# Query and key projections by seven products of quarters instead of eight, in three PSUM banks

## The chip, the cores and the metric

The kernel runs on one core of a Trainium2 chip. The metric is the time of one execution on the device in microseconds (us). A core has five engines that work side by side, each through its own list of instructions in order: TensorE (PE, matmuls; its weight loads are listed apart as PEld), VectorE (DVE), ScalarE (ACT), GpSimd (POOL) and SyncE (SP, which issues most DMA transfers). They meet at semaphores. Matmuls write PSUM, which has banks of 128 partitions by 512 float32; everything else is in SBUF.

## The reference, cut to what matters

An input x of 2 batches of 1024 tokens and 1024 features is normalized and goes through one attention layer and, beside it, a gated feed-forward layer whose weights are stored in 4 bits. The change lies in the projections ahead of the attention:

```
h = layernorm(x)                       # (2, 1024, 1024)
q = rope(h @ wq)                       # 32 heads of 32, 1024 columns
k = rope(h @ wk)                       # 8 heads of 32, 256 columns
v = h @ wv                             # 256 columns, no rope
attention = softmax(q @ k.T / sqrt(32), causal) @ v @ wo
```

Four query heads share a key head. Rope turns neighbouring columns of a head by an angle that depends on the token: t * cos + swapped(t) * sin.

## The kernel before, in words

The two batches go one after the other through the stages "normalize", `project`, `attend` and `project_out`; the feed-forward layer comes last, for both. The stage that the change touches is `project`, called once a batch.

Normalized activations stand transposed in `xnT`: features on the partitions, in NS = 8 slices of 128, and 1024 tokens along the row, taken as two blocks of TB = 512. The weights of 128 columns are a tile of 8 slices of 128x128. For one block of 128 columns and 512 tokens, a **group**, PE runs eight float32 matmuls 128x512, one for each slice, that add up in one bank (L384). Three banks called ps_qk take turns. Keys have two blocks of columns, queries eight (NC), each with two blocks of tokens: 20 groups a batch, 160 matmuls.

After each group comes its **turn** (L386 to L398): DVE multiplies the bank by the cosines (L388) and shuffles neighbouring rows of the bank (L390), POOL multiplies the shuffled copy by the sines (L391) and adds the two (L392), ACT makes a rounded copy, `rot_hi` (L394), DVE subtracts it to get the rest, `rot_lo` (L396), and SP stores both to a DRAM buffer of queries or keys, `qs` or `ks` (L397, L398). From there the attention fetches them as stacks of rows, `room_*`.

Three other things are woven into `project`:

- `work`, the row maxima for the first group of heads (`head.rows()`): products of queries and keys, called s (L548 and L554), in two banks of their own, each followed by a DVE reduce (L564); 42 of these groups a batch. One is drawn after every second matmul of a query group from the third block of columns on. They need the first stacks, fetched after the keys and after the first query block (`head.keys()`, `head.queries()`).
- `side`: in batch 0 a survey of the 4-bit scales and zero points (`look`), whose transfers zb_gu (8) and zb_d (21) are issued from ACT's queue; in batch 1 the unpacking of 4-bit weights (`unpack`, DVE L258 to L263, ACT L267, POOL's transfers L249). `behind(turn)` asks the scheduler to put these behind the turn.
- after each query block, the split of one slice of xnT into x_hi (ACT, L439) and x_lo (DVE, L440), stored for the feed-forward layer.

At the end the values: 8 groups ps_v of 8 matmuls 128x256 (L407), copied out by ACT (L410).

Weights come from a pool of three tiles (`load_w`), loaded two blocks ahead. The order of instructions on each engine is set by a scheduler from the order of the program and these hints. `room` is nine tiles of 128x1024, allocated at once (L1457); the last four are filled only in `attend`. `oT`, where the attention leaves its result, is 128x8x1024 and idle during `project` (L1450).

Of the kernel before, what the change touches and what calls it, by code (L numbers as in the profile page):

```python
# [10 lines left out]
F32 = mybir.dt.float32  # L11
F32R = mybir.dt.float32r
# [5 lines left out]
AF = mybir.ActivationFunctionType  # L18
ALU = mybir.AluOpType
# [4 lines left out]
P = 128  # L24
# [8 lines left out]
NREP = N_HEADS // N_KV  # L33
# [3 lines left out]
def block_kernel(  # L37
# [18 lines left out]
    nc = tc.nc  # L56
# [288 lines left out]
    def load_w(pool, w_dram, c, **kw):  # L345
        return load_w_at(pool, w_dram, c, **kw)[0]
# [5 lines left out]
    def load_kv(pool, w_dram, w=None):  # L352

        if w is None:
            w = pool.tile([P, NS, N_KV * HD], F32, name="w_kv")
        nc.sync.dma_start(w, w_dram.rearrange("(g p) n -> p g n", p=P))
        return w

    def project(b, xnT, w_k, qs, ks, v, side, head):


        with tc.tile_pool(name="qkv_w", bufs=3, reuse_waits="tile") as wp, tc.tile_pool(name="qkv", bufs=3, reuse_waits="tile") as pool, tc.tile_pool(
            name="qkv_t", bufs=1, reuse_waits="tile"
        ) as tp, tc.tile_pool(name="qkv_ps", bufs=3, space=PSUM, reuse_waits="tile") as psp, tc.tile_pool(
            name="v_ps", bufs=2, space=PSUM, reuse_waits="tile"
        ) as vps, tc.tile_pool(name="x_split", bufs=2, reuse_waits="tile") as xp:
            cs = tp.tile([P, 2, T], F32, name="cs")
            for j in range(4):
                nc.sync.dma_start(cs[HD * j : HD * (j + 1)], rope.rearrange("a d t -> d a t"))
            swap = [i ^ 1 for i in range(32)]  # L370

            def behind(turn):

                order = ExitStack()
                for i in turn:
                    order.enter_context(tc.issue_after(i.ins))
                return order

            def turned(w, dst, work=iter(()), blocks=range(NB)):
                for n in blocks:  # L380
                    tok = slice(n * TB, (n + 1) * TB)
                    ps = psp.tile([P, TB], F32, name="ps_qk")
                    for s in range(NS):
                        nc.tensor.matmul(ps, w[:, s, :], xnT[:, s, tok], start=(s == 0), stop=(s == NS - 1))  # L384
                        if s % 2:
                            next(work, None)  # L386
                    t1 = pool.tile([P, TB], F32, name="rot1")
                    nc.vector.tensor_tensor(t1, ps, cs[:, 0, tok], ALU.mult)  # L388
                    t2 = pool.tile([P, TB], F32, name="rot2")
                    nc.vector.stream_shuffle(t2, ps, swap)  # L390
                    nc.gpsimd.tensor_tensor(t2, t2, cs[:, 1, tok], ALU.mult)  # L391
                    turn = [nc.gpsimd.tensor_tensor(t1, t1, t2, ALU.add)]  # L392
                    hi = pool.tile([P, TB], F32R, name="rot_hi", bufs=2)
                    turn.append(nc.scalar.copy(hi, t1))  # L394
                    lo = pool.tile([P, TB], F32R, name="rot_lo", bufs=2)
                    turn.append(nc.vector.tensor_tensor(lo, t1, hi.bitcast(F32), ALU.subtract))  # L396
                    nc.sync.dma_start(dst[0, :, tok], hi.bitcast(F32))  # L397
                    nc.sync.dma_start(dst[1, :, tok], lo.bitcast(F32))  # L398
                    with behind(turn):
                        for _ in range(3 if b else 1):  # L400
                            next(side, None)
                return turn
# [9 lines left out]
            wanted = list(range(NC))  # L412
            loaded = [load_w(wp, wq, wanted.pop(0)) for _ in range(2)]
            def following():
                if wanted:
                    loaded.append(load_w(wp, wq, wanted.pop(0)))
                return loaded.pop(0)


            for n in range(NB):  # L420
                for c in range(2):
                    turned(w_k[:, :, c * P : (c + 1) * P], ks[c], blocks=[n])
            w = load_kv(None, wv, w_k)
            head.keys()
            work = head.rows()
            for c in range(NC):
                turn = turned(following(), qs[c], work if c > 1 else iter(()))
                if c == 0:
                    head.queries()
                if c == NC - 2:  # L430

                    warm = tp.tile([P, 1], F32, name="warm")
                    nc.scalar.activation(warm, eps, AF.Exp)
                for n in range(NB):
                    tok = slice(n * TB, (n + 1) * TB)
                    hi = xp.tile([P, TB], F32R, name="x_hi")
                    lo = xp.tile([P, TB], F32R, name="x_lo")
                    with behind(turn):
                        nc.scalar.copy(hi, xnT[:, c, tok])  # L439
                        nc.vector.tensor_tensor(lo, xnT[:, c, tok], hi.bitcast(F32), ALU.subtract)  # L440
                    nc.sync.dma_start(xs_dram[b][0, :, c, tok], hi.bitcast(F32))
                    nc.sync.dma_start(xs_dram[b][1, :, c, tok], lo.bitcast(F32))

            for t in range(NT):
                next(work, None)
                values(t)
            for _ in work:
                pass
# [5 lines left out]
    class Clock:  # L454
# [6 lines left out]
        def product(self, w, n=1.0, switch=False):  # L461
            self.pe += 15.0 + 0.416 * n * w + (90.0 if switch else 0.0)
# [984 lines left out]
    for b in range(B):  # L1447
        keep_open = ExitStack()
        keep = keep_open.enter_context(tc.tile_pool(name="keep", bufs=1, reuse_waits="tile"))
        oT = keep.tile([P, NS, T], F32, name="oT")  # L1450
        q0_open = ExitStack()
        q0p = q0_open.enter_context(tc.tile_pool(name="at_q0", bufs=1, reuse_waits="tile"))
        with tc.tile_pool(name="at_first", bufs=1, reuse_waits="tile") as fp, tc.tile_pool(
            name="qkv_T", bufs=1, reuse_waits="tile"
        ) as qp:

            room = [q0p.tile([P, T], F32R, name=f"room_{j}") for j in range(1 + 2 * NREP)]  # L1457
            v = qp.tile([P, NT, N_KV * HD], F32, name="v")
            with tc.tile_pool(name="ps_s", bufs=1, space=PSUM, reuse_waits="tile") as ps_s:
                head = Maxima(qs_dram[b], ks_dram[b], fp, ps_s, room)  # L1460
                if b == 0:
                    with tc.tile_pool(name="prep", bufs=1) as pool, tc.tile_pool(
                        name="prep_ps", bufs=1, space=PSUM
                    ) as psp:
                        first = look(pool, psp)
                        project(b, xnT, w_k, qs_dram[b], ks_dram[b], v, first, head)
                        for _ in first:
                            pass
                else:
                    with tc.tile_pool(name="unpack", bufs=2, side="right", reuse_waits="tile") as up:  # L1470
                        side = unpack(up, range(8, 20), False)
                        project(b, xnT, w_k, qs_dram[b], ks_dram[b], v, side, head)
                        for _ in side:
                            pass
                x_open.close()
                output = Output(b, oT, q0p)
                attend(head, v, oT, output)
        if b == B - 1:
            ffn_args = start_ffn(ffn_open)
            xnT = xp = None  # L1480
        else:
            x_open, xnT, xp = open_x()
        with tc.tile_pool(name="unpack", bufs=3, side="right", reuse_waits="tile") as up:
            side = unpack(up, range(8) if b == 0 else range(20, NF), b == B - 1)
# [62 lines left out]
```

## Time and profile before

| what | value |
|---|---|
| runs of the kernel | 2291.7, 2293.06, 2296.47 us; median 2293.06 us |
| profiled execution | 2293.33 us, its span 2291.6 us |
| granted TensorE clock, mean | 0.993 |
| `project`, batch 0, first ps_qk to last ps_v | 26.9 to 220.4 us |
| `project`, batch 1, the same | 667.8 to 852.9 us |
| one group of 8 matmuls, PE, by the timeline | 6.87 us |

The span runs from the first to the last instruction. Rows of the profile name a line of the kernel, the engine, the operation, what it writes and reads, and the shape; then busy time in us and mean ns of one, then idle time ahead of it on its engine and what ended that. A float32 matmul leaves two records, so 160 matmuls a batch show as 320. Matmul records overlap, so that their mean is longer than the distance from one to the next.

### The profile page before, as it was taken

The numbers are of one execution on the slowest core, as the hardware profiler recorded it, in microseconds if no ns is written. First come the engines' busy times: TensorE is split into PE (matmuls) and PEld (weight loads), VectorE is DVE, ScalarE is ACT, GpSimd is POOL, SyncE is SP. The second block draws the span as 40 slices with busy tenths as digits, with TensorE's granted clock in tenths as the row PEclk, the third lists the DMA queues.
The fourth block names the chain that finished last, engine by engine and source line by source line (L and its number), as shares of the span: only waits on it lengthen the run. The fifth ranks groups of instructions, "written<-read, shape, count | busy, mean of one in ns | idle before, by whom it ended". The sixth has DMA issues, their size and how long they took to land.

```text
span 2291.6 us, 30825 instructions
## 1 busy us (share of the span) xinstructions
PE 2239.3 (98%) x11313; PEld 1537.5 (67%) x11313; DVE 1420.2 (62%) x2268; ACT 1132.3 (49%) x1819; POOL 792.4 (35%) x569
## 2 busy tenths in 40 slices
PE   7989999999999999999999999999999999999998
PEld 4455555555874465555558888888877888888875
DVE  5544677773324736777722367667877777777775
ACT  2102544553223325445533455555887555556875
POOL 1303677774035427776741100000234100001362
PEclk9999999999999999999999999999999999999999
DMA  5727323122468971231319623231846655323475
GB/s 180 220 91 244 80 47 93 38 75 76 129 210 280 301 215 47 52 88 38 80 54 344 181 56 83 55 83 55 303 138 219 176 137 139 96 71 105 137 231 154
DMA packets 262183, 309.50 MB, mean 135 GB/s; under 512 B 19147, under 2 KB 197707, under 8 KB 261880
## 3 DMA queue, kind: packets, MB, share of 16 engines
q1 hardware_dynamic: 245172, 260.62, 38.4%
q0 software_dynamic: 10752, 38.02, 5.2%
q10 hardware_dynamic: 6100, 8.82, 1.2%
q8 instruction: 91, 1.49, 0.3%
q14 instruction: 68, 0.56, 0.1%
HBM read 214.58 MB, written 97.03 MB: 136 GB/s over the span
## 4 chain that ended last, share of the span: by engine, by line
PE 82%; issue 7%; POOL 6%; DVE 2%; ACT 2%; DMA 1%; SPq 0%; ACTq 0%; POOLq 0%; DVEq 0%
PE acc L1198 27%; PE acc L1079 12%; PE ps_wo L880 10%; PE st L661 7%; PE s L554 7%; PE o L708 5%; PE ps_qk L384 5%; PE l L726 3%; PE st L676 2%; PE ps_v L407 1%; POOL rot L391 1%; PE s L548 1%; POOL rot L392 1%; POOL p L821 1%; ACT p L686 1%
## 5 line engine op out<-in xcount | busy, mean ns | idle before, releaser
L1198 PE MATMUL acc<-x,w 128*128 128x512 f32 x2752 | 640.1, 393 | 1.2 <-ACT gate L1169 0.9
L1198 PEld LDWEIGHTS acc<-x,w 128*128 128x128 f32 x2752 | 512.3, 188 | 120.5 <-DVE h L1171 7.2
L564 DVE TENSOR_REDUCE mx<-s 128x1 f32<-128x512 f32 (+3 forms) x672 | 384.8, 608 | 190.3 <-PE s L554 91.7
L968 DVE TENSOR_SCALAR acc<-acc,r_gu 128x1024 f32<-128x1024 f32 x301 | 389.1, 1293 | 166.5 <-PE acc L1198 164.9
L686 ACT ACTIVATE p<-st 128x512 f32<-128x512 f32 (+3 forms) x768 | 314.7, 497 | 316.8 <-PE st L676 314.6
L966 ACT ACTIVATE acc<-acc,r_gu 128x1024 f32<-128x1024 f32 x301 | 327.4, 1088 | 231.5 <-PE acc L1198 226.7
L1182 POOL TENSOR_TENSOR h_lo<-h,h_hi 128x512 fp32r<-128x512 f32 x78 | 100.3, 1287 | 805.2 <-DVE h L1160 300.6
L821 POOL TENSOR_TENSOR p<-p 128x2048 f32<-128x2048 f32 (+3 forms) x122 | 360.0, 2955 | 9.0 <-PE o L708 4.6
L968 DVE TENSOR_SCALAR acc<-acc,r_d 128x512 f32<-128x512 f32 x320 | 241.7, 759 | 62.0 <-PE acc L1079 59.3
L966 ACT ACTIVATE acc<-acc,r_d 128x512 f32<-128x512 f32 x320 | 210.8, 663 | 61.8 <-PE acc L1079 55.0
L384 PE MATMUL ps_qk<-xnT,w_qk 128*128 128x512 f32 x512 | 236.0, 602 | 2.5 <-DVE rot L390 2.5
L880 PE MATMUL ps_wo<-oT,w_o 128*128 128x256 f32 x1024 | 232.1, 382 | 0.0
L1079 PE MATMUL acc<-h_lo,w 128*128 128x512 f32 (+1 forms) x576 | 228.9, 397 | 3.0 <-POOL h_lo L1182 2.6
L1079 PE MATMUL acc<-h_hi,w 128*128 128x512 f32 (+1 forms) x576 | 229.5, 398 | 0.7 <-ACT h_hi L1181 0.7
L880 PEld LDWEIGHTS ps_wo<-oT,w_o 128*128 128x128 f32 x1024 | 191.1, 190 | 40.9 <-issue 16.7
L708 PE MATMUL o<-p,v 128*32 128x512 f32 (+3 forms) x1536 | 162.9, 496 | 0.9 <-POOL p L689 0.9
L384 PEld LDWEIGHTS ps_qk<-xnT,w_qk 128*128 128x128 f32 x512 | 94.6, 192 | 99.8 <-issue 93.4
L689 POOL TENSOR_SCALAR_AFFINE_SELECT p<-p 128x512 f32<-128x512 f32 x128 | 80.5, 636 | 163.5 <-ACT p L686 123.0
L391 POOL TENSOR_TENSOR rot<-rot,cs 128x512 f32<-128x512 f32 x40 | 51.3, 1283 | 239.6 <-DVE rot L390 230.2
L554 PE MATMUL s<-kst,room 128*128 128x512 f32 (+3 forms) x384 | 130.4, 379 | 0.0
L1079 PEld LDWEIGHTS acc<-h_lo,w 128*128 128x128 f32 (+1 forms) x576 | 108.4, 188 | 31.0 <-POOL h_lo L1182 5.4
L1079 PEld LDWEIGHTS acc<-h_hi,w 128*128 128x128 f32 (+1 forms) x576 | 108.3, 188 | 30.6 <-issue 2.9
(163 smaller groups left out, 2405.7 us busy)
## 6 DMA issues: line engine op xcount, KB each, us to landing
w<-ng SPq DMA_DIRECT2D x86, 512.0 KB, 5.2
w<-nd SPq DMA_DIRECT2D x63, 512.0 KB, 4.0
ng<-nf POOLq DMA_DIRECT2D x42, 512.0 KB, 6.9
room<-qs SPq DMA_DIRECT2D x160, 128.0 KB, 4.0
x<-xs SPq DMA_DIRECT2D x32, 512.0 KB, 10.2
qst<-qs SPq DMA_DIRECT2D x96, 128.0 KB, 3.8
xt<-in_L_attn_x SPq DMA_DIRECT2D x16, 512.0 KB, 6.2
w_qk<-in_L_attn_wq SPq DMA_DIRECT2D x16, 512.0 KB, 5.0
```

The source lines that it names most:

```text
L384: nc.tensor.matmul(ps, w[:, s, :], xnT[:, s, tok], start=(s == 0), stop=(s == NS - 1))
L554: nc.tensor.matmul(s[:, c * w : (c + 1) * w], q[j][:, qt * P : (qt + 1) * P], k[:, k0:k1], start=n == 1, stop=c == n - 1 and (n > 1 or not ...
L564: nc.vector.tensor_reduce(mx[:, at, js[0] : js[0] + n, k0 // TB], s[:, : w * n].rearrange("p (j t) -> p j t", j=n), AX.X, ALU.max)
L661: nc.tensor.matmul(s[:, q0:], kst[g][:, kt * P : (kt + 1) * P], stack[g][j][:, qlo + q0 : qlo + TB], start=True, stop=False,)
L686: nc.scalar.activation(p[:, j, q0:], st[j][:, q0:], AF.Exp, scale=1.0 / math.sqrt(HD))
L708: nc.tensor.matmul(o[HD * j : HD * (j + 1), q0:], v[:, kt, HD * g : HD * (g + 1)], p[:, j, q0:], start=(kt == 0), stop=last,)
L821: what(*args)
L880: self.last = nc.tensor.matmul(ps[:, c * self.BLK : (c + 1) * self.BLK], self.ws[c0 + c][:, g, :], self.oT[:, g, t0 : t0 + self.BLK], star ...
L966: nc.scalar.mul(a, a, r)
L968: nc.vector.tensor_scalar(a, a, r, None, ALU.mult)
L1079: nc.tensor.matmul(acc[c], w[:k, c * P : (c + 1) * P], ht[:k, :], start=(f == 0 and t == 0), stop=(t == 1), skip_group_check=(f > 0),)
L1198: nc.tensor.matmul(a[:, n, :], w[i][:, g * P : (g + 1) * P], xs[t][:, g, n * TB : (n + 1) * TB], start=(g == 0 and t == 0), stop=(t == 1), ...
```

## The change

One level of Strassen's scheme, in Winograd's form, is put in place of the plain product. Two blocks of columns, `wa` and `wb`, the slices 0 to 3 and 4 to 7, and the two blocks of tokens make a 2x2 by 2x2 product of quarters, each quarter product being four matmuls. Instead of 8 quarter products for such a pair there are 7, on sums of quarters:

- Four sums of activations, S, of 128x2048 each, once a batch, on DVE. They stand in `oT`.
- Four sums of weights a pair (`quarters`), two on DVE and two on POOL, 128x512 each; one overwrites the lower half of `wb`.
- The products P1, P5, P2, P6, P3, P7, P4 in that order, in three banks: P1 and then P2 in ps_0, P5 and then P3 in ps_2, P6, P7 and P4 in ps_1. The later ones in a bank add to what is there, after it was copied or read: ACT copies P1 and P5 to SBUF, POOL adds them (p5), DVE adds P6 and P1 (u2). Three more DVE sums (`sum_of`) make the other three of a pair's four results: the turn of the first reads its bank, the other three read SBUF.
- P1 of a pair stands ahead of P4 of the one before, and the pair's last turn and the x split follow P4.
- Keys are the first pair, queries the next four: five pairs a batch. `work` starts at the third pair.
- rot1 and rot2 have two buffers, not three. `behind` holds for `side` in batch 1 only.
- Query weights are loaded into the places of stacks, `room_5` to `room_8`, a pair ahead; the four stacks are allocated after `project`.

```diff
-            def turned(w, dst, work=iter(()), blocks=range(NB)):
-                for n in blocks:
-                    tok = slice(n * TB, (n + 1) * TB)
-                    ps = psp.tile([P, TB], F32, name="ps_qk")
-                    for s in range(NS):
-                        nc.tensor.matmul(ps, w[:, s, :], xnT[:, s, tok], start=(s == 0), stop=(s == NS - 1))
-                        if s % 2:
+            H = NS // 2
+            A = {(n, k): xnT[:, k * H : (k + 1) * H, n * TB : (n + 1) * TB] for n in range(2) for k in range(2)}
+            S = [S[:, 2 * i : 2 * i + 2, :].rearrange("p a (b t) -> p (a b) t", b=2) for i in range(4)]
+            for out, x, y, op in (
+                (S[0], A[1, 0], A[1, 1], ALU.add),
+                (S[1], S[0], A[0, 0], ALU.subtract),
+                (S[3], A[0, 1], S[1], ALU.subtract),
+                (S[2], A[0, 0], A[1, 0], ALU.subtract),
+            ):
+                nc.vector.tensor_tensor(out, x, y, op)
+
+            def quarters(wa, wb):
+
+                low, high = slice(0, H), slice(H, NS)
+                t = [wp.tile([P, H, P], F32, name=f"t_{i}") for i in range(3)]
+                nc.vector.tensor_tensor(t[0], wb[:, low], wa[:, low], ALU.subtract)
+                nc.vector.tensor_tensor(t[1], wb[:, high], t[0], ALU.subtract)
+                nc.gpsimd.tensor_tensor(wb[:, low], wb[:, high], wb[:, low], ALU.subtract)
+                nc.gpsimd.tensor_tensor(t[2], wa[:, high], t[1], ALU.subtract)
+                return {1: wa[:, low], 2: wa[:, high], 3: wb[:, high], 4: t[2], 5: t[0], 6: t[1], 7: wb[:, low]}
...
+            def pair(B, dsts, work, done):
...
+                def product(i, x, bank, first):
+                    if first:
+                        banks[bank] = psp.tile([P, TB], F32, name=f"ps_{bank}", bufs=1)
+                    for s in range(H):
+                        nc.tensor.matmul(
+                            banks[bank], B[i][:, s, :], x[:, s, :], start=first and s == 0, stop=s == H - 1,
+                            skip_group_check=not first,
+                        )
+                        if s % 2 and i > 1:
                             next(work, None)
...
+                def sum_of(bank, y):
+                    nc.vector.tensor_tensor(y, banks[bank], y, ALU.add)
+                    return y
+
+                p1, p5, u2 = part("p1"), part("p5"), part("u2")
+                product(1, A[0, 0], 0, True)
+                nc.scalar.copy(p1, banks[0])
+                yield
+                product(5, S[0], 2, True)
+                nc.scalar.copy(p5, banks[2])
+                nc.gpsimd.tensor_tensor(p5, p1, p5, ALU.add)
+                yield
+                product(2, A[0, 1], 0, False)
+                turn_heads(banks[0], 0, dsts[0])
+                yield
+                product(6, S[1], 1, True)
+                nc.vector.tensor_tensor(u2, banks[1], p1, ALU.add)
+                yield
+                product(3, S[3], 2, False)
+                turn_heads(sum_of(2, u2), 0, dsts[1])
+                yield
+                product(7, S[2], 1, False)
+                turn_heads(sum_of(1, p5), 1, dsts[1])
+                yield
+                product(4, A[1, 1], 1, False)
+                done(turn_heads(sum_of(1, p1), 1, dsts[0]))
+                yield
...
+            def weights(i):
+                return [load_w(places, wq, c, tag=f"room_{1 + NREP + c % 4}") for c in (2 * i - 2, 2 * i - 1)]
+
+            work = head.rows()
+            PAIRS = 1 + NC // 2
+            loads = [[w_k[:, :, :P], w_k[:, :, P:]], weights(1)]
+            B = quarters(*loads[0])
+            running = None
+            for i in range(PAIRS):
+                dsts = (ks[0], ks[1]) if i == 0 else (qs[2 * i - 2], qs[2 * i - 1])
+                g = pair(B, dsts, work if i > 1 else iter(()), lambda turn, i=i: done(i, turn))
+                next(g)
+                for _ in running or ():
+                    pass
+                if i == 1:
+                    w = load_kv(None, wv, w_k)
+                if 0 < i < PAIRS - 1:
+                    loads.append(weights(i + 1))
+                for _ in range(4):
+                    next(g)
+                if i + 1 < PAIRS:
+                    B = quarters(*loads[i + 1])
+                next(g)
+                running = g
+            for _ in running:
+                pass
...
-            room = [q0p.tile([P, T], F32R, name=f"room_{j}") for j in range(1 + 2 * NREP)]
+            room = [q0p.tile([P, T], F32R, name=f"room_{j}") for j in range(1 + NREP)]
...
+                room += [q0p.tile([P, T], F32R, name=f"room_{j}") for j in range(1 + NREP, 1 + 2 * NREP)]
```

`turn_heads(c, n, dst)` is the turn of before for one block, on a source `c` that is a bank or a tile in SBUF; `split_x` and `done` hold what followed each query block before.

More of the change, by code (lines that the diff above doesn't have):

```diff
@@ L357, in load_kv, with project @@
         return w
-    def project(b, xnT, w_k, qs, ks, v, side, head):
-        with tc.tile_pool(name="qkv_w", bufs=3, reuse_waits="tile") as wp, tc.tile_pool(name="qkv", bufs=3, reuse_waits="tile") as pool, tc.tile_pool(
+    def project(b, xnT, w_k, qs, ks, v, side, head, S, places):
+        with tc.tile_pool(name="qkv_w", bufs=1, reuse_waits="tile") as wp, tc.tile_pool(name="qkv", bufs=2, reuse_waits="tile") as pool, tc.tile_pool(
             name="qkv_t", bufs=1, reuse_waits="tile"
@@ L377, in behind @@
                 return order
-            def turned(w, dst, work=iter(()), blocks=range(NB)):
-                for n in blocks:
-                    tok = slice(n * TB, (n + 1) * TB)
-                    ps = psp.tile([P, TB], F32, name="ps_qk")
-                    for s in range(NS):
-                        nc.tensor.matmul(ps, w[:, s, :], xnT[:, s, tok], start=(s == 0), stop=(s == NS - 1))
-                        if s % 2:
-                            next(work, None)
[L387 to L402, printed above, removed]
@@ new lines, in turn_heads @@
+            def turn_heads(c, n, dst):
+                tok = slice(n * TB, (n + 1) * TB)
+                t1 = pool.tile([P, TB], F32, name="rot1")
+                nc.vector.tensor_tensor(t1, c, cs[:, 0, tok], ALU.mult)
+                t2 = pool.tile([P, TB], F32, name="rot2")
+                nc.vector.stream_shuffle(t2, c, swap)
+                nc.gpsimd.tensor_tensor(t2, t2, cs[:, 1, tok], ALU.mult)
+                turn = [nc.gpsimd.tensor_tensor(t1, t1, t2, ALU.add)]
+                hi = pool.tile([P, TB], F32R, name="rot_hi")
+                turn.append(nc.scalar.copy(hi, t1))
+                lo = pool.tile([P, TB], F32R, name="rot_lo")
+                turn.append(nc.vector.tensor_tensor(lo, t1, hi.bitcast(F32), ALU.subtract))
+                nc.sync.dma_start(dst[0, :, tok], hi.bitcast(F32))
+                nc.sync.dma_start(dst[1, :, tok], lo.bitcast(F32))
+                with behind(turn) if b else ExitStack():
+                    for _ in range(3 if b else 1):
+                        next(side, None)
+                return turn
@@ new lines, in pair, with part @@
+            def pair(B, dsts, work, done):
+                banks = {}
+                def product(i, x, bank, first):
[7 more added lines that the diff above has]
+                        if s % 2 and i > 1:
+                            next(work, None)
+                def part(name):
+                    return pool.tile([P, TB], F32, name=name, bufs=1)
+                def sum_of(bank, y):
[24 more added lines that the diff above has]
+                yield
@@ L410, in values, with split_x @@
                 nc.scalar.copy(v[:, t, :], ps)
[L412 to L433, printed above, removed]
+            def split_x(c, turn):
                 for n in range(NB):
@@ L442, in project, with done @@
                     nc.sync.dma_start(xs_dram[b][1, :, c, tok], lo.bitcast(F32))
+            def done(i, turn):
+                if i == 0:
+                    head.keys()
+                if i == 1:
+                    head.queries()
+                if i == NC // 2 - 1:
+                    warm = tp.tile([P, 1], F32, name="warm")
+                    nc.scalar.activation(warm, eps, AF.Exp)
+                for c in (2 * i - 2, 2 * i - 1) if i else ():
+                    split_x(c, turn)
+            def weights(i):
[11 more added lines that the diff above has]
+                    pass
+                if i == 1:
+                    w = load_kv(None, wv, w_k)
[9 more added lines that the diff above has]
+                pass
             for t in range(NT):
@@ L1465, in block_kernel @@
                         first = look(pool, psp)
-                        project(b, xnT, w_k, qs_dram[b], ks_dram[b], v, first, head)
+                        project(b, xnT, w_k, qs_dram[b], ks_dram[b], v, first, head, oT, q0p)
                         for _ in first:
@@ L1471, in block_kernel @@
                         side = unpack(up, range(8, 20), False)
-                        project(b, xnT, w_k, qs_dram[b], ks_dram[b], v, side, head)
+                        project(b, xnT, w_k, qs_dram[b], ks_dram[b], v, side, head, oT, q0p)
                         for _ in side:
```

## The prediction

> **What bounds the kernel now.** I read the page's totals first, then its chain, then the two stages in which the changed function runs.
>
> ```profile
> span 2291.6 us, 30825 instructions
> PE 2239.3 (98%) x11313; PEld 1537.5 (67%) x11313; DVE 1420.2 (62%) x2268; ACT 1132.3 (49%) x1819; POOL 792.4 (35%) x569
> PE 82%; issue 7%; POOL 6%; DVE 2%; ACT 2%; DMA 1%; SPq 0%; ACTq 0%; POOLq 0%; DVEq 0%
> ```
>
> TensorE is busy 98% of the span and carries 82% of the chain: matmul time taken out counts in full, as long as the others keep up. Whether they do is read from the two stages, given here as windows (start and end, length, then busy time and instruction count of PE, PEld, DVE, ACT, POOL, granted clock, DMA share, GB/s).
>
> ```profile
> 24.00:225.00 201.00, 192.43 (x590) 104.38 (x588) 92.54 (x218) 29.03 (x53) 52.19 (x43) 0.96 0.52 168
> 668.00:855.00 187.00, 181.03 (x542) 96.77 (x541) 92.00 (x204) 50.18 (x71) 71.06 (x64) 1.00 0.78 244
> 156.00:160.00 4.00, 3.01 (x4) 1.46 (x5) 0.94 (x3) 0.00 (x0) 2.52 (x2) 0.50 0.28 98
> ```
>
> In both, PE is nearly full and DVE half full. By its timeline the first stage runs from 26.9 (first ps_qk) to 220.4 us (last ps_v), 193.5 us, and then waits 2.4 us for qst; the second from 667.8 to 852.9, 185.1 us. The last row is a stretch after PE had stood idle for 3.9 of the 5 us before it: the clock is at 0.50. An idle PE is paid for twice.
>
> The rows by form price every operation (busy us, mean ns; then idle before and its releaser):
>
> ```profile
> L384 PE MATMUL ps_qk<-xnT,w_qk 128*128 128x512 f32 x512 | 236.0, 602 | 2.5 <-DVE rot L390 2.5
> L388 DVE TENSOR_TENSOR rot<-ps_qk,cs 128x512 f32<-128x512 f32 x40 | 27.4, 686 | 33.5 <-PE ps_qk L384 33.5
> L390 DVE STREAM_SHUFFLE rot<-ps_qk 128x512 f32<-128x512 f32 x40 | 29.0, 726 | 0.0
> L391 POOL TENSOR_TENSOR rot<-rot,cs 128x512 f32<-128x512 f32 x40 | 51.3, 1283 | 239.6 <-DVE rot L390 230.2 <-issue 9.4
> L392 POOL TENSOR_TENSOR rot<-rot,rot 128x512 f32<-128x512 f32 x40 | 51.0, 1275 | 3.1
> L396 DVE TENSOR_TENSOR rot_lo<-rot,rot_hi 128x512 fp32r<-128x512 f32 x40 | 27.9, 697 | 93.4 <-ACT rot_hi L394 91.3 <-DMA xs<-x_lo 2.1
> ```
>
> Of these the last is the one to look at: DVE stands 93.4 us over 40 turns, 2.3 us a turn, at rot_lo, because its own shuffle must first go through two POOL operations and an ACT copy (1.28+1.28+0.62 and handoffs, 3.37 us where nothing lies between). Today that costs nothing: three banks rotate and PE waited 2.5 us in all.
>
> **What is removed.** A key or query group is 8 matmuls, two records each at 0.43 us apart in the timeline: 6.87 us. A pair of column blocks is four groups, 27.5 us; after the change seven products of 4 matmuls, 7 x 3.44 = 24.1 us. Five pairs a batch: 17.2 us, two batches: 34.4 us off PE. The order of the changed kernel does hold 140 such matmuls a batch for 160. If all of it came through, 2293.3 - 34.4 = 2258.9 us.
>
> **What is added.** Per pair, at the row durations: DVE two quarters, u2 and three sum_of, 6 x 0.69 = 4.1 us; POOL two quarters and p5, 3 x 1.28 = 3.8 us; ACT two copies, 1.2 us. Per batch four S sums of 128x2048 on DVE; no row has that form. The nearest ones, reduces of 256, 384 and 512 columns at 421, 548 and 684 ns, grow by 1.03 ns a column, which makes 2.3 us each (from 4 x 0.684 = 2.7 down to 2.0 as bounds). So DVE gets about 30 us a batch on 92, POOL 19 on 52 or 71. Neither is full by that; the order decides.
>
> **The DVE queue, pair by pair.** DVE works in order. In a plain pair of batch 1 its list reads: turn, (unpack) u2 (unpack) quarter sum, turn with a sum inside, unpack, turn, unpack sum, turn with a quarter inside, unpack, x_lo. A turn is 0.69+0.73, the wait, 0.70. With the mean wait of 2.3 it is 4.4 us, with the bare one of 3.37 it is 5.5. Four turns 17.7 to 22; u2, one quarter and two sums outside the turns 2.8; four x_lo 2.8; unpack 3.8 (0.29+0.29+0.38 four times). That is 27 to 31 us against PE's 24.1 (before: 24 to 29 against 27.5, with three free banks between). **The wait moves to PE**: u2 frees bank 1 for P7 and the sums free banks for P4, P5 and P6, and all stand in this queue behind rot_lo. Each pair would then last about 29 us, 5 more than its matmuls and 1.5 more than now.
>
> **The sum.** I laid both orders out instruction by instruction, each starting when its engine, its operands and its bank or buffer are free, with these durations. Batch 1: before 183.6 (185.1 in the trace), PE busy 176.0; after, PE busy 158.8 and 27 us of waits (14.6 on u2, p1 and the sums, 12 on row-maxima reduces), 185.7 us: **+2**. Batch 0: before 181.2, after 190.9. The trace has 195.9 there with the qst wait, 14.7 more than my layout: about 2 is the slow start of the clock, 2.4 the qst wait, and 10 the ACT queue, which is stuck for 20.3 and 45.1 us issuing the zb transfers. In the new order those issues are spread ahead of the turns, and the query stacks are fetched much earlier. I let the qst wait go and half of the 10 stay: 190.9+2+5 = 198, **+2**.
>
> In batch 0 there is one more thing. 38 or so row-maxima products stand in one block ahead of P2 of the third query pair, with few ps_v matmuls between. They follow each other on PE every 0.2 to 0.3 us where nothing holds them, the reduce of each takes 0.42 to 0.68: some 29 us for 11 us of matmuls. The layout contains these 18 us of idling; it doesn't contain the clock. By the 156 to 160 row a half-idle PE drops to 0.50; the block's 11 us and what follows would gain 0 to 8 us, I take **+4**, near the middle, since here PE gets a matmul every 0.7 us, where it had none for 2.5 us in that row.
>
> Sum: +2 +2 +4 = +8 on the profiled execution's 2293.3 (span 2291.6 and 1.7 around it), 2301. The median shown, 2293.06, is the same time.
>
> **Costed at nothing.** Query weights now go to the places of stacks, a pair ahead: 24 us of cover for a transfer that lands in 5.0 us. Two stacks of attend wait for the last query products, some 40 us before they are used. Value weights overwrite w_k after the last key product, a stage's length before use. The SP queue carries the same transfers; stores come in bursts of a pair rather than singly, behind each other by 0.4 us an issue. ACT's p1 copy gates P2: behind a zb issue it would hold PE, up to the 20 us of one such block; I leave that in the range. With rot1 and rot2 in two buffers rather than three, the next multiply waits for the copy of the turn before the last: inside the 5.5 us of a turn.
>
> **A rule against a row.** DVE and POOL get in each other's way here (start, duration):
>
> ```profile
> 532.68 4.57 POOL L821 TENSOR_TENSOR p<-p 128x2048 f32<-128x2048 f32 x1 [2.31 <-PE o L708]
> 533.64 4.15 DVE L753 TENSOR_TENSOR oT<-oc,rt 128x512 f32<-128x512 f32 x1
> ...
> 1192.95 0.69 DVE L753 TENSOR_TENSOR oT<-oc,rt 128x512 f32<-128x512 f32 x1
> ```
>
> The same DVE operation takes 0.69 us alone and 4.15 us when begun inside a POOL operation, ending 0.5 us after it. The Trainium skill, "SBUF — State Buffer", section "SBUF: two separate sides", calls the port pair of the two an exclusive lock: a DVE operation with two SBUF inputs and a GpSimd operation that reads SBUF exclude each other for a whole instruction, whoever starts second waits. It speaks against this change: quarters, S, rot_lo and x_lo all have two SBUF inputs, and three of the four turn multiplies of a pair, which read PSUM before, now read u2, p5 and p1 in SBUF, while POOL works 14 us of each 24 (11 operations). By the stretch that before's stages show (x_lo 748 ns on average against 684 undisturbed, 2 us in 32) the lock would cost 2 to 4 us; by the rule, in my layout, 9 in batch 1 and some 6 in batch 0. I take the rule, since the row above shows it at full size and the exposed operations multiply. Without it the sum is 2301 - 15 + 3, near 2289.
>
> **Rivals.**
> - *Saving mostly kept*, 2259 to 2275: DVE's waits fall beside each other and PE never sees them. For it: DVE is idle half of the stage. Against it: 27 us of in-order work for 24 of PE. 0.08.
> - *Partly kept, faster*, 2276 to 2288, typically 2283: no lock at work in the pairs, and the zb block of batch 0 dissolves wholly. It decides once the DVE chain of a pair is below 27.5 us: each us under that is 10 us over the ten pairs, down to PE's own 24.1. For it: the 10 us that ACT loses today; against it: the row at 533.64. 0.20.
> - *Given back with little over*, 2289 to 2308, likeliest 2301: 0.45, of which 0.17 lie below 2298.
> - *Clearly slower*, 2309 to 2325: the DVE chain at the bare 31 us in all pairs (2 us more in each of ten, 20 us), or p1 behind zb issues, and a clock at half in the maxima block. 0.25.
> - *It doesn't do what it says*: the matmuls not fewer, only DVE work more, above 2320. The order with its 140 matmuls a batch speaks against it. 0.02.
>
> A measurement of this kernel tells 0.2%, 4.6 us, from no change. Faster: 0.08+0.20 = 0.28; same, 2288.5 to 2297.7: 0.17; slower: 0.55. The range, 2275 to 2320, leaves out the first case and the far end of the slow one, some 0.16 together.
>
> **What would show it.** In the changed profile: PE's busy time lower by some 34 us, with PE idle in front of product matmuls released by DVE (u2, the sums) and by reduces, some 25 us a stage; DVE's multiplies and quarters longer than 0.69 us on average; rot_lo still waiting 2 to 3.4 us; the clock below 1 in a maxima block of batch 0. The prediction is wrong if PE's idle time before the products stays below 5 us a stage, if DVE's waits at rot_lo fade, or if the two stages change by different signs. The rest (attend, output, FFN) should not change by more than 1 us.

## The result, and the profile after

| what | before | after |
|---|---|---|
| median of the runs | 2294.47 us | 2317.89 us |
| ratio | | 1.0101, 95% interval 1.0083 to 1.0118 |
| profiled execution, its span | 2293.33, 2291.6 | 2317.56, 2315.8 |
| first product of batch 0 | 26.9 | 28.7 |
| stage of batch 0 (first product to the attention's first product, st) | 193.5 | 205.9 |
| from there to batch 1's first product | 447.4 | 444.2 |
| stage of batch 1 | 185.1 | 195.2 |
| rest of the span | 1438.7 | 1441.8 |

The changed kernel is 1.0% slower, 23 us, although 40 of 320 product matmuls are gone from PE. The lower five rows are read off the timeline of the profiled execution. They sum to the span and say where: 12.4 us in batch 0's stage, 10.1 in batch 1's, 1.8 before and 3.1 behind, less 3.2 between.

The page's totals and its chain:

```profile
span 2315.8 us, 30821 instructions
PE 2228.9 (96%) x11233; PEld 1529.2 (66%) x11233; DVE 1501.8 (65%) x2336; ACT 1144.4 (49%) x1839; POOL 838.4 (36%) x599
PE 77%; DVE 5%; POOL 5%; DMA 5%; issue 4%; ACT 2%; SPq 1%; ACTq 0%; POOLq 0%; DVEq 0%
```

PE's share of the chain fell from 82% to 77%, and DVE's rose from 2% to 5%. DMA's rose from 1% to 5%, but its longest pieces, 41 us of loads zt<-zb_d, lie near 1260 to 1300 us in the feed-forward layer, outside the two stages. PE's busy time fell by 10.4 us only, not by 34. The windows of the stages tell why (columns as in the prediction). Before:

```profile
26.90:220.40 193.50, 187.05 (x565) 100.01 (x564) 92.23 (x217) 23.56 (x44) 51.77 (x42) 0.97 0.50 165
667.80:852.90 185.10, 179.13 (x532) 95.59 (x530) 92.00 (x204) 48.51 (x68) 71.06 (x64) 1.00 0.78 244
```

After, with two slices of batch 0:

```profile
28.70:234.60 205.90, 183.87 (x526) 96.89 (x524) 132.19 (x242) 29.36 (x55) 71.12 (x53) 0.90 0.51 164
678.80:874.00 195.20, 171.01 (x492) 89.24 (x490) 129.53 (x235) 53.99 (x79) 91.65 (x77) 0.97 0.73 226
140.00:160.00 20.00, 16.92 (x40) 9.94 (x40) 16.00 (x29) 3.69 (x8) 2.53 (x2) 0.50 0.38 124
160.00:180.00 20.00, 15.47 (x36) 7.49 (x36) 11.88 (x27) 1.76 (x3) 2.87 (x2) 0.72 0.30 117
```

Length less busy is PE's idle time: 6.5 and 6.0 us before, 22.0 and 24.2 after. The busy time should have fallen by 17.2 us in each stage; it fell by 3.2 and 8.1. So 14.0 and 9.1 us of it are missing, and the clock column names a part: 0.90 and 0.97 of full speed where it was 0.97 and 1.00. The stretches at half clock, in the same columns, are a long one in batch 0 (a short one follows at 195 us) and three in batch 1:

```profile
133.70:171.20 37.50, 26.99 (x61) 15.06 (x62) 27.97 (x57) 3.69 (x8) 2.53 (x2) 0.50 0.43 135
714.00:717.40 3.40, 3.25 (x4) 1.50 (x5) 0.26 (x1) 1.01 (x3) 3.32 (x4) 0.50 0.45 127
744.70:751.50 6.80, 5.34 (x7) 2.25 (x8) 3.65 (x10) 3.36 (x6) 5.33 (x5) 0.50 0.66 192
836.90:840.30 3.40, 3.12 (x5) 1.71 (x6) 3.13 (x7) 0.00 (x0) 1.62 (x3) 0.50 1.01 315
```

PE is busy at half clock for 30.4 us in batch 0 (10.7 before) and for 11.7 in batch 1 (none before). By an estimate, if work at half clock takes twice its time, half of that is lost: some 10 us more than before in batch 0 and 6 in batch 1. The other 4 and 3 us of the missing time are not accounted for.

**Batch 1: the ring.** The next P2 needs the copy of P1, the copy needs the buffer p1 free, and p1 comes free with the last sum and turn of the pair before: a ring through three engines. Stretches of the timeline, DVE, then ACT's copy of P1, then PE, then POOL (start, duration; in brackets idle time and what ended it):

```profile
702.88 0.29 DVE L258 TENSOR_SCALAR nib<-qw 128x512 uint16<-128x512 uint16 x1
...
704.36 0.72 DVE L409 STREAM_SHUFFLE rot<-p 128x512 f32<-128x512 f32 x1
708.46 1.27 DVE L415 TENSOR_TENSOR rot_lo<-rot,rot_hi 128x512 fp32r<-128x512 f32 x1 [3.37 <-ACT rot_hi L413]
709.64 1.35 DVE L260 TENSOR_SCALAR nib<-qw 128x512 uint16<-128x512 uint16 x1
711.03 0.42 DVE L263 TENSOR_TENSOR nib<-nib,zt 128x512 uint16<-128x512 uint16 x1
711.37 0.68 DVE L442 TENSOR_TENSOR p<-ps,p 128x512 f32<-128x512 f32 x1
712.09 0.69 DVE L407 TENSOR_TENSOR rot<-p,cs 128x512 f32<-128x512 f32 x1
...
713.51 0.59 ACT L447 COPY p<-ps 128x512 f32<-128x512 f32 x1 [0.97 <-DVE rot L409]
...
714.15 5.30 PE L431 MATMUL ps<-xnT,w_qk 128*128 128x512 f32 x8 [4.24 <-ACT p L447]
...
709.32 1.52 POOL L400 TENSOR_TENSOR t<-w_qk,t 128x512 f32<-128x512 f32 x1
```

DVE stands 3.37 us at rot_lo; rot_lo then takes 1.27 us for 0.69, beside two transfers that POOL issues (L249, from 707.71 us), and the unpack operation behind it 1.35 us for 0.29, beside POOL's quarter sum. Only then come the sum and the turn that free p1, and ACT's copy of the next P1, for which P2 waits. PE stands 4.24 us. The two stretched operations add some 1.6 us; the wait of 3.37 us ahead of them in the same queue is the larger part.

**Batch 0: the block of maxima.** From ACT and PE:

```profile
117.90 29.00 ACTq L223 DMA_DIRECT2D zb_d<-z_d  x17
146.94 0.62 ACT L413 CAST rot_hi<-rot 128x512 fp32r<-128x512 f32 x1 [30.42 <-DMA zb_d<-z_d]
147.47 0.58 ACT L447 COPY p<-ps 128x512 f32<-128x512 f32 x1
...
167.95 0.61 PE L685 MATMUL m_ps<-ident_b,mt 128*128 128x128 bf16 x4 [2.65 <-DVE mt L674]
168.35 5.11 PE L431 MATMUL ps<-xnT,w_qk 128*128 128x512 f32 x8
```

ACT does nothing else for 30.4 us, until the zb transfers on its queue are out (the row begins at 118 us and counts the last 17). Behind them stand a rot_hi and the copy of P1, which is done at 148.1 us; P2 needs the copy. But P2 starts at 168.35, 20 us later: PE's list has all remaining row maxima in front of it. From 128.9 to 168.4 us PE does nothing else, at the pace of DVE's reduces and from 133.7 on at half clock, 39.5 us. So in this execution it is the order of PE's list, not the late copy, that holds P2.

### The profile page after: what moved, and what is told of

Read it like the earlier page. It is cut to its first block, busy times and chain, and to the rows that moved or that the text cites. A ratio compares the mean times of both kernels' runs of the same rounds, so it can differ in the third digit from the quotient of the medians.

```text
span 2315.8 us, 30821 instructions
## 1 busy us (share of the span) xinstructions
PE 2228.9 (96%) x11233; PEld 1529.2 (66%) x11233; DVE 1501.8 (65%) x2336; ACT 1144.4 (49%) x1839; POOL 838.4 (36%) x599
## 4 chain that ended last, share of the span: by engine, by line
PE 77%; DVE 5%; POOL 5%; DMA 5%; issue 4%; ACT 2%; SPq 1%; ACTq 0%; POOLq 0%; DVEq 0%
PE acc L1284 27%; PE acc L1165 12%; PE s L640 7%; PE st L747 7%; PE ps_wo L966 6%; PE o L794 5%; PE ps L431 4%; PE l L812 3%; PE st L762 2%; DMA zt<-zb_d 2%; PE s L634 1%; POOL p L907 1%; PE ps_v L472 1%; POOL rot L410 1%; POOL rot L411 1%
## 5 line engine op out<-in xcount | busy, mean ns | idle before, releaser
L747 PE MATMUL st<-room,kst 128*128 128x512 f32 (+3 forms) x384 | 119.2, 371 | 3.2 <-ACT p L772 3.2
L413 ACT CAST rot_hi<-rot 128x512 fp32r<-128x512 f32 x40 | 24.7, 617 | 177.2 <-POOL rot L411 139.0
L267 ACT ACTIVATE nf<-nib 128x1024 fp32r<-128x1024 uint8 (+2 forms) x68 | 68.2, 1040 | 88.7 <-DVE nib L263 41.3
```

The costliest lines, as they stand in the source:

```text
L747: nc.tensor.matmul(s[:, q0:], kst[g][:, kt * P : (kt + 1) * P], stack[g][j][:, qlo + q0 : qlo + TB], start=True, stop=False,)
```

## The experiments

Stages are read off one profiled execution each; ratios are to the kernel before, run on the same chip.

| run | median us | ratio, 95% interval | batch 0 | between | batch 1 |
|---|---|---|---|---|---|
| before | 2294 | 1 | 193.5 | 447.4 | 185.1 |
| changed kernel | 2317.89 | 1.0101, 1.0083 to 1.0118 | 205.9 | 444.2 | 195.2 |
| before, zb later | 2301.73 | 1.0031, 1.0021 to 1.0040 | 184.4 | 464.0 | 185.4 |
| changed, zb later | 2313.72 | 1.0086, 1.0069 to 1.0102 | 182.1 | 463.6 | 194.5 |
| changed, rot_lo later | 2300.19 | 1.0030, 1.0017 to 1.0042 | 198.8 | 444.3 | 185.8 |
| changed, two p1 | 2319.82 | 1.0111, 1.0094 to 1.0127 | 205.2 | 444.4 | 199.0 |
| before, zb merged | 2291.47 | 0.9985, 0.9978 to 0.9992 | 189.4 | 448.8 | 185.0 |
| changed, both (e6) | 2279.35 | 0.9936, 0.9920 to 0.9953 | 179.5 | 443.6 | 187.3 |
| e6, x splits apart | 2283.13 | 0.9955, 0.9938 to 0.9972 | 183.8 | 443.7 | 186.7 |
| changed, sums in PSUM | 2314.94 | 1.0088, 1.0071 to 1.0105 | 200.6 | 444.0 | 198.7 |
| changed, zb merged | 2301.14 | 1.0032, 1.0020 to 1.0045 | 189.0 | 443.8 | 195.3 |
| e6, POOL's sums on DVE | 2275.08 | 0.9921, 0.9904 to 0.9937 | 180.4 | 443.9 | 181.7 |
| e6, slower unpacking | 2288.89 | 0.9977, 0.9970 to 0.9984 | 179.7 | 443.8 | 191.7 |
| changed, POOL's sums on DVE | 2322.37 | 1.0117, 1.0100 to 1.0134 | 207.9 | 444.1 | 196.6 |

### The zb transfers later

```diff
-            nc.scalar.dma_start(zb_gu[r0:r1], z_gu[g : g + 1].to_broadcast([r1 - r0, 2 * INTER, 2]))
-            nc.scalar.dma_start(zb_d[r0:r1], z_d[g : g + 1].to_broadcast([r1 - r0, D, 2]))
+    def spread_zeros():
...
+            nc.sync.dma_start(zb_gu[r0:r1], z_gu[g : g + 1].to_broadcast([r1 - r0, 2 * INTER, 2]))
...
+            nc.sync.dma_start(zb_d[r0:r1], z_d[g : g + 1].to_broadcast([r1 - r0, D, 2]))
...
                         for _ in first:
                             pass
+                        spread_zeros()
```

In the kernel before:

> The kernel before, with the 29 zb transfers taken off ACT's queue in batch 0's projection and issued by SP after it. In this kernel no query or key matmul waits for ACT. Theory (ACT's blocked queue matters only once the copies P1 and P5 stand on it): the stage of batch 0 stays within 4 us of 193.5, the total within 5 of 2293. Rival (the queue costs both kernels the same): the stage falls by about 10 us, the total to 2283.

In the changed kernel:

> The changed kernel with the same move of the zb transfers. Theory (the copy of P1 waits in ACT's queue behind zb issues for about 30 us, PE meanwhile has only row maxima to do, at the pace of the reduces and then at half clock): the block of maxima between 129 and 168 us dissolves, clock at 1.0 in all of batch 0's slices but the first two or three, stage from 206 to about 188 us, total near 2300. Rival (DVE is too full in any case, the waits only move): stage not below 200, total above 2310.

Without the transfers on ACT the changed kernel's stage falls by 23.8 us, that of before by 9.1. So the theory is right for the changed kernel's stage, and its first half is wrong: before paid for the queue too, about as much as the prediction had put down (10 us); by its trace a rot_hi stood there 19.8 us and an x_hi 50.7 behind these transfers. Both totals miss their theories: before gets 7 us slower (1.0031), and the changed kernel gains 4 us where 18 were forecast, as the attention now waits for its first query stacks: "between" grows by 17 to 19 us. Its row in the waits of PE (us in all, times, longest) in the changed kernel with zb later:

```profile
PE s L640 <- DMA qst<-qs: 17.3, 4, 12.1
```

The stages answer the question, the totals don't.

### rot_lo behind the next bank read

```diff
-                lo = pool.tile([P, TB], F32R, name="rot_lo")
-                turn.append(nc.vector.tensor_tensor(lo, t1, hi.bitcast(F32), ALU.subtract))
+                def rest(after=()):
+                    lo = pool.tile([P, TB], F32R, name="rot_lo")
+                    with behind(after):
+                        turn.append(nc.vector.tensor_tensor(lo, t1, hi.bitcast(F32), ALU.subtract))
...
-                turn_heads(banks[0], 0, dsts[0])
+                rest, _ = turn_heads(banks[0], 0, dsts[0])
                 yield
                 product(6, S[1], 1, True)
-                nc.vector.tensor_tensor(u2, banks[1], p1, ALU.add)
+                read = nc.vector.tensor_tensor(u2, banks[1], p1, ALU.add)
+                rest([read])
...
-                turn_heads(sum_of(2, u2), 0, dsts[1])
+                rest, _ = turn_heads(sum_of(2, u2), 0, dsts[1])
...
+                last, read = turn_heads(sum_of(1, p5), 1, dsts[1])
+                rest([read])
...
+                rest, read = turn_heads(sum_of(1, p1), 1, dsts[0])
+                last([read])
+                done(rest())
```

`turn_heads` now returns `rest` and its shuffle, `read`. The store of rot_lo and the steps of `side`, in batch 1 the unpacking, are drawn in `rest` too and so move with it.

> The changed kernel with rot_lo of three of the four turns of a pair put behind the next bank read or shuffle on DVE. Theory (DVE standing at rot_lo holds up u2 and the sums, and so PE): batch 1's stage from 195 to about 186 us, PE's wait for the copy of P1 (9.9 us there) mostly gone, total 8 to 12 below the changed kernel's 2318. Rival (the number of DVE and POOL operations binds, not their order): less than 3 us.

Not one operation more or less, and 17.7 us are back: 9.4 in batch 1, 7.1 in batch 0. The theory stands, the rival falls. DVE's wait at rot_lo in batch 1, in the changed kernel and in this run, and what PE still waits for there:

```profile
DVE rot_lo L415 <- ACT rot_hi L413: 39.1, 15, 3.4
...
DVE rot_lo L419 <- ACT rot_hi L413: 12.0, 7, 2.8
...
PE s L649 <- DVE mx L659: 11.1, 7, 2.9
PE ps L436 <- DVE u L462: 3.3, 2, 2.2
PE ps L436 <- ACT p L452: 1.6, 1, 1.6
```

PE's wait for the copy of P1 fell from 8.3 to 1.6 us (the 9.9 of the expectation is that of its weight loads), the one for reduces stayed (11.5 before the edit). In batch 0 DVE's wait at rot_lo fell from 21.5 to 10.6 us, while the block of maxima stands as it did, from 128.7 to 166.8 us: the 7.1 us there are not the block's. How much of the gain belongs to rot_lo and how much to the unpack steps that moved with it was not separated.

### Two buffers for p1

```diff
-                p1, p5, u2 = part("p1"), part("p5"), part("u2")
+                p1, p5, u2 = part("p1", 2), part("p5", 1), part("u2", 1)
```

> The changed kernel with two buffers for p1, so that the copy of a pair's P1 needn't wait until the last turn of the pair before has read the old p1. Theory (a ring P4, sum, turn, copy, P2 through the one buffer is where DVE's delay reaches PE): PE's wait for that copy (9.9 us in batch 1, 4.1 in batch 0) goes, total 8 to 12 below 2318. Rival (DVE late all the same, the wait moves to P4 and P6 or to the maxima): less than 4 us.

Nothing gained, and batch 1's stage is 3.8 us longer. PE's waits of batch 1 show the rival at work, though at another place than it named: the wait for p1 is gone, and the next reader of a bank in DVE's late queue, u2, for which P7 waits, takes its place, 12.9 us where it had been 3.0:

```profile
PE ps L431 <- DVE u L457: 12.9, 2, 6.6
PE s L640 <- DVE mx L650: 11.0, 8, 3.3
```

The second buffer lets ACT copy earlier; it doesn't make DVE's queue any shorter.

### The zb transfers merged, 3 for 29, on ACT's queue

```diff
-        for g in range(G_GU):
...
+        nc.scalar.dma_start(
+            zb_gu.rearrange("(g r) d i -> g r (d i)", g=G_GU),
+            z_gu.rearrange("g d i -> g (d i)").rearrange("g (o n) -> g o n", o=1).to_broadcast([G_GU, P // G_GU, 4 * INTER]),
+        )
```

and likewise for the rows of zb_d, with one more for its last group. In the kernel before:

> The kernel before, with the 29 zb transfers of batch 0 merged into 3 on the same queue, ACT's, at the same place (the two runs with them later took 9 and 24 us off batch 0's stage but gave 17 to 19 back between the stages, where the attention waited for qst behind them on SP). Theory: ACT is no longer held by 29 issues in turn; stage of batch 0 from 193.5 to about 185 us, nothing given back, total near 2285. Rival (what holds is the bytes of these transfers, not their number): stage not below 191.

Stage 189.4, between theory and rival: 4.1 us gained, of which 1.4 go between the stages. The total gains 0.15%, at an interval that ends at 0.9992.

What the queue was held by is neither the bytes nor the issues as such. In the kernel before, the 29 issues take 0.5 to 0.6 us each (the last 1.3), some 17 us of the 65; the rest are waits. By the trace each of these transfers waits for a semaphore that it shares with earlier transfers, of SP's queue too, until those have landed. The two longest waits, 16.1 us up to 138.0 and 15.3 up to 157.6, end with the landing of a w_qk and of a qs<-rot_lo that SP had issued 4.7 and 2.0 us before; the longest in the changed kernel, 12.7 us up to 133.7, with that of a qs<-rot_hi. Three transfers have fewer places at which to wait.

In the changed kernel, together with the later rot_lo:

> The changed kernel with rot_lo behind the next bank read (as in the third run, 2300) and the merged zb transfers. Theory (the two causes add): stage of batch 0 from 198.8 to about 178 us, batch 1 stays at 186, total near 2279, below the kernel before (2294) and 6 below the kernel before with the same merge. Rival (in batch 0 the reduces and DVE's list bind as in batch 1): stage of batch 0 about 186, total about 2287, no faster than the kernel before with the merge.

As the theory had it, 2279.35, and batch 0's stage 179.5. In batch 1 the stage stays 2.2 us above that of before. And the merge alone:

> The changed kernel with the merged zb transfers alone (rot_lo in its old place). Theory (two causes that add: ACT's queue in batch 0, rot_lo's place in both batches): stage of batch 0 about 186 (205.9 less the 19 that the merge took in e6 against e3), batch 1 195, total about 2298. Rival (the merge works only where DVE's list is eased): stage of batch 0 above 195.

189.0 us for 205.9, 16.8 off the total, both 3 us short of the theory but far below the rival's 195. The same slices as above, in this run:

```profile
140.00:160.00 20.00, 18.32 (x52) 8.71 (x51) 16.33 (x36) 3.94 (x7) 7.54 (x5) 0.91 0.80 275
160.00:180.00 20.00, 17.52 (x46) 8.59 (x47) 14.53 (x28) 4.68 (x8) 8.62 (x7) 0.91 0.47 165
```

The clock no longer sits at half. On PE's list the 57 maxima in a row of the changed kernel have become runs of 1 to 5 between products. The block stands in every version of the changed kernel that keeps the 29 transfers on ACT's queue (with one break where the sums go to PSUM), and in none of those that merge or move them. That the scheduler puts the maxima in front because it reckons with ACT's queue is argued from this, not shown. The two edits take 17.7 and 16.8 us alone and 38.5 together: they add, with some 4 us more.

### Around the best of these

```diff
-                for c in (2 * i - 2, 2 * i - 1) if i else ():
-                    split_x(c, turn)
+                    if splits and all(dst is not k for k in ks):
+                        c_x, n_x = splits.pop(0)
+                        split_x(c_x, turn, [n_x])
```

> As the run before (e6), and the four x splits of a pair no longer in a row after its last turn but one after each turn. Theory (in the third run DVE stood up to 3.2 us at x_lo, whose two buffers wait for their stores, and the reduces and with them PE stood behind): batch 1's stage 3 to 6 us shorter than e6's, batch 0's 2 to 4. Rival (x_lo's waits lie beside others): within 2 us of e6.

Not so: batch 1 gains 0.6, as the rival had it, and batch 0 loses 4.3, which neither had and which stays open.

On e6 again, the unpacking:

```diff
-                    for _ in range(3 if b else 1):
+                    for _ in range(2 if b else 1):
```

> As e6, with two instead of three steps of the 4-bit unpacking drawn a turn in batch 1; the rest follows after the projection. Theory (in batch 1 DVE's list, 140 us busy of 187, is what PE waits for: the unpack operations, held by POOL up to 3 us, are a part of it): batch 1's stage 4 to 7 us shorter, of which some 2 come back in the attention. Rival (PE waits for the row maxima whatever lies between): stage within 2 us of 187.3.

Both are wrong: the stage grew by 4.4 us. PE's waits there now hold 9.1 us of ps_v on ACT's v, behind the unpack steps that are drawn after the last turn; the work was moved to where the matmuls have no cover left.

### The port of DVE and POOL

```diff
-                    nc.vector.tensor_tensor(y, banks[bank], y, ALU.add)
-                    return y
+                    to = banks[bank] if last else y
+                    nc.vector.tensor_tensor(to, banks[bank], y, ALU.add)
+                    return to
```

with `last` for the sums of P3 and P4:

> The changed kernel with two of a pair's three sum_of written back to their bank, so that two of the three multiplies on SBUF read PSUM again (same count and size). Theory (the shared port: with one SBUF input such a multiply is not held up by POOL): these multiplies at 0.69 us, POOL's rope operations 1.28 on average for 1.32, batch 1's stage 2 to 4 us shorter. Rival (banks are held 1.4 us longer, which costs more than the port): stage longer than 195.

The multiplies on SBUF of the changed kernel and one of its quarters, by form (busy us, mean ns), and then the multiplies of this run:

```profile
L407 DVE TENSOR_TENSOR rot<-p,cs 128x512 f32<-128x512 f32 x20 | 16.9, 847 | 0.3
...
L398 DVE TENSOR_TENSOR t<-w_qk,t 128x512 f32<-128x512 f32 x8 | 9.0, 1121 | 2.7 <-PE ps L431 2.6
...
L407 DVE TENSOR_TENSOR rot<-u,cs 128x512 f32<-128x512 f32 x10 | 6.9, 687 | 0.2
```

```profile
L407 DVE TENSOR_TENSOR rot<-ps,cs 128x512 f32<-128x512 f32 x30 | 20.5, 684 | 5.5 <-PE ps L431 5.1
L407 DVE TENSOR_TENSOR rot<-p,cs 128x512 f32<-128x512 f32 x10 | 8.5, 851 | 0.1
```

On p, with two inputs in SBUF, the multiply is stretched to 847 ns, and the quarter to 1121. On u, with two as well, it is not, at 687; that POOL seldom meets it there is argued. From PSUM a multiply takes 684 ns. But batch 1's stage is 3.5 us longer, on the rival's side: PE waits 9.3 us for u2 (3.0 before), as banks are held for longer. It also waits 3.1 us for a load of w_qk, which cost the changed kernel at most 0.5, so that the run does not weigh port against banks cleanly. POOL's operations are no shorter (1.33 us). Batch 0 gains 5.3 us with another order of the list, in which the block of maxima is broken once, and says nothing of the port.

```diff
-                nc.gpsimd.tensor_tensor(wb[:, low], wb[:, high], wb[:, low], ALU.subtract)
-                nc.gpsimd.tensor_tensor(t[2], wa[:, high], t[1], ALU.subtract)
+                nc.vector.tensor_tensor(wb[:, low], wb[:, high], wb[:, low], ALU.subtract)
+                nc.vector.tensor_tensor(t[2], wa[:, high], t[1], ALU.subtract)
...
-                nc.gpsimd.tensor_tensor(p5, p1, p5, ALU.add)
+                nc.vector.tensor_tensor(p5, p1, p5, ALU.add)
```

First on e6, then on the changed kernel:

> As e6, with the three POOL sums of a pair (two quarters, p5) on DVE: DVE gets 2.1 us a pair more, POOL 3.8 less (the POOL operations that take 1.3 to 1.5 us). Theory (the port: a POOL operation can hold DVE for its 1.3 us, on DVE the same costs 0.7): DVE's quarters and rot_lo at 0.7 to 0.8 us, stages of e6 1 to 4 us shorter. Rival (DVE's count of operations binds): each stage 3 to 8 us longer, total near 2290.

> The changed kernel with its three POOL sums of a pair on DVE and nothing else. Theory (POOL's sums cost twice, in the turn's path through POOL and by holding DVE at the port): 4 to 8 us below the changed kernel's 2318, mostly in batch 1's stage, as in e10 against e6. Rival (with rot_lo in its old place DVE's list is already the longer one, and 10 us more on it cost): 2318 or up to 8 above.

On e6 it brings 5.6 us in batch 1 (x_lo 712 ns for 843, the first quarter 702 for 1020), in the total 4 us, at the edge of the intervals: the best version seen, 0.9921 of before. On the changed kernel as it stands it brings nothing (2322.37, the rival's side), although there too DVE's operations get shorter (the second quarter 742 ns for 1121): DVE idles 58.0 us in front of rot_lo as it did (60.6), and the freed time seems to be idled away there. The stretch beside POOL is real, second in rank, and its share of the 23 us is not settled beyond that: the two rope operations of each turn stayed on POOL in both runs.

## Why the prediction was right, and where it was off

**The direction and the mechanism.** Forecast 2301, slower; measured 2317.9, inside the range of 2275 to 2320, near its upper end, and 23 us above before where 8 were forecast. The step that carried it, "the wait moves to PE", because rot_lo stands in DVE's queue ahead of u2 and the sums, is shown by the third run, which moves rot_lo and what is drawn with it. The direction owes something to luck. Without the lock at full size the sum would have been near 2289, faster than before, and no run shows the lock to cost 15 us. The clock, put at +4 and in one block only, cost more: by the estimate above some 10 and 6 us. If the lock costs less than 15, errors of opposite sign have put the forecast on the right side.

**PE's waits.** "27 us of waits" in batch 1: 24.2 of idling measured. Of its parts, reduces, forecast 12, measured 11.7; u2, p1 and sums 14.6, measured 11.6 by PE's rows.

**The signs it named.** PE's idle time (22.0 and 24.2 us a stage for "some 25"), the longer multiplies and quarters, and the low clock in batch 0's block came. PE's busy time fell by 10.4 us instead of 34. DVE's wait at rot_lo did not fade, but shrank from 93.4 to 60.6 us, 1.5 a turn instead of 2 to 3.4. The rest of the kernel changed by some 3 us on either side of batch 1 rather than by 1 at most.

**Batch 1's +2 was +10.** The layout set the clock at 1.00 and came near the waits; the trace had 0.97, with 20 us slices of 0.91, 0.83 and 0.92. PE's busy time fell by 8.1 us for 17.2. That is the term that was mis-sized: the prediction charged the clock in the maxima block alone, and by the estimate above some 6 of the 9 missing us are the clock's here as well. The other 3 stay open.

**Batch 0's +6 was +9.2** (205.9 and the 3.2 less between, against 193.5). "+4" for the clock was too small, since the block held 57 maxima, not "38 or so", and lasted 39.5 us, not 29, at half clock from 133.7 to 171.2 us. ACT's queue, of whose cost the prediction let 5 us stay and left the rest to the range, was the main thing: with the transfers out of the way the stage falls by 17 to 24 us. But it did not come as the remark had it, p1's copy "behind a zb issue would hold PE, up to the 20 us": the copy was done 20 us before PE came to P2, and what goes with the transfers is the block on PE's list. The 10 us that before loses to that queue were right in size by the first run, 9.1; the merge gained 4.1.

**The rule of the port** (the Trainium skill, "SBUF — State Buffer", section "SBUF: two separate sides"), taken at 15 us. The operations stretch in the direction that it says: 847 ns for 687 in one form, 1121 in another that takes 742 once POOL's sums are gone. That the time follows at this size is not shown: moving POOL's sums brought 4 us once and none once. Between rule and row, 2 to 15 us, it stays open; the order of the queue was the larger matter.

**Costed at nothing.** Query weights: 0.5 us of wait in batch 1, right. rot1, rot2: no wait seen. Not foreseen: 1.8 us ahead of the first product. Most of it goes when POOL's sums move to DVE: the first product starts at 28.7 us in the changed kernel and at 27.1 and 27.0 in those two runs, although DVE then has all four key quarters among the normalization's operations. In the changed kernel two of DVE's operations there took 1.65 and 1.31 us beside POOL's two quarters, for 0.64 and 0.80 without. Nor were the 3.1 us behind batch 1, whose attention starts with a qst wait of 1.6 us and a clock of 0.83 in its first 10 us.

**Rivals.** "Partly kept, faster" is what the edited kernel does at 2279, and at 2275 it comes to the edge of "mostly kept": a part of the saving was to be had, by order rather than by less work. Against before with the same merge, 2291, seven products are worth 12 to 16 of the 34 us. The move of rot_lo was not tried in before, where PE had waited 2.5 us in all for its product banks. What holds back the other 18 to 22 us is open; in batch 1 PE still waits some 11 us for reduces.

## What to carry to other kernels

When matmuls are saved by sums on other engines, count the longest queue in order, not the busy shares: DVE was busy for two thirds of the stage and still set the pace, because an operation that waits for two other engines stood ahead of those that free PE's banks. Try such an operation behind the reads that release banks; here it cost nothing and gave back 17.7 us. When a copy on a so far idle engine becomes part of PE's path, look at what else that engine's queue holds, transfers included, and at what those wait for.

## What the runs showed that was not expected

- 29 small transfers on one queue held it for 65 us in the kernel before, some 48 of them in waits for earlier transfers to land, of another queue too; 3 that move the same bytes were issued in 0.7 to 1.2 us each.
- PE's list kept 57 row maxima in front of a product whose operand had been ready for 20 us.
- Moving the 29 to another engine's queue and a later place saved 9 to 24 us there and cost 17 to 19 us later, with the first loads of the next stage behind them.
- Adding a buffer moved 8 us of PE's wait from one releaser to another without a gain.
- A 16-bit operation of the unpacking on DVE, 0.29 us alone, took 1.35 us beside a POOL sum.
